# Attention probabilities on their way through DRAM: stores on ScalarE's queue, loads on SyncE's, both in program order

## The chip, the cores and the metric

The kernel runs on one core of a Trainium2 chip. A core has five engines with an instruction stream each: TensorE (PE in the profile, its weight loads as PEld), VectorE (DVE), ScalarE (ACT), GpSimd (POOL) and SyncE (SP). Each stream runs in order. A transfer between memories is an instruction on one of these streams, which only issues it; 16 DMA engines shared by all streams then move the bytes, and the stream goes on. A stream stands still at an instruction whose inputs aren't ready, an issue of a transfer too, and everything behind it on that stream waits as well. The metric is the time of one execution on the device in microseconds, the median of several.

## The reference

Four blocks run after one another: a cross-attention with injected context, a time-mixing layer with a scan, a decoder layer with two attentions, and a non-local block. The change touches the two attentions of the third block, batch 8, sequence 256, width 512, 16 heads of 32:

```python
def attention(q, k, v, mask):
    scores = jnp.einsum('bhqd,bhkd->bhqk', q, k) / jnp.sqrt(jnp.float32(HD))
    scores = scores * mask - 10000.0 * (1.0 - mask)
    probs = jax.nn.softmax(scores, axis=-1)
    return jnp.einsum('bhqk,bhkd->bhqd', probs, v)

ln_out = layernorm(hidden_states, ln1_s, ln1_b)
qkv = ln_out @ w_qkv + b_qkv
q, k, v = jnp.split(qkv, 3, axis=-1)
x = hidden_states + merge_heads(attention(heads(q), heads(k), heads(v), ltor_mask)) @ w_ao + b_ao
ln_out = layernorm(x, ln2_s, ln2_b)
q = ln_out @ w_q + b_q
k, v = jnp.split(encoder_states @ w_kv + b_kv, 2, axis=-1)
x = x + merge_heads(attention(heads(q), heads(k), heads(v), cross_mask)) @ w_co + b_co
```

All of it is computed in float32. The first attention has one mask for all batches, the second a mask and an encoder block per batch.

## The kernel before

**Tiling.** A run i is one batch of one attention: runs 0 to 7 are the first attention (`a_`), runs 8 to 15 the second (`c_`). A run has four iterations, one for each group ct of four heads, so there are 64 iterations; each falls into two halves of two heads. A half is one tile of probabilities, 128 partitions by 4 rows of 256.

**One half** passes through these steps:
- `scores` (L1119, PE): 16 matmuls for the whole iteration, into four PSUM tiles `sp`.
- `masked` (L1131 and L1134, DVE): scale and mask, then add the mask term `mb` and take the row maximum `nmax`; result `pe`.
- `exps` (L1143, ACT): four exponentials with their row sums.
- `divided` (L1151 DVE, L1153 POOL): reciprocals of the sums, then four multiplications on POOL.
- `turn` (L1163 to L1169): DVE transposes `pe` in blocks of 32 by 32 into `dt`; a transfer stores `dt` to a DRAM buffer (L1167, 512 KB of traffic); four transfers load it back from there, with another order of the partitions, into `pt` (L1169, 128 KB each). Each half has a DRAM buffer of its own; `dt` has six buffers, `pt` a tag of its own for each half of an iteration.
- `values` (L1182, PE): 16 matmuls of the iteration with the values `av`. The first four records read the first half's `pt` alone, the other twelve need the second half's as well. ACT moves the result into `cx` (L1186).

**Order.** The main loop (L1278 to L1299) writes, for each step n: the scores of iteration n+1; then for the two halves k of that iteration `masked(k)`, `exps(k)`, `divided(k-1)` and `turn(k-2)`; then other work that has come due; then the values of iteration n-1. The steps of masking, exponentials, division and the transposes are wrapped in `pin`, which is `keep_in_program_order`: among themselves they stay in the order written. A scheduler places everything else among them by its own estimates of times. The stores L1167 and the loads L1169 aren't pinned and are issued from SyncE.

**The other work** of a run, by a table of due times (L1223 to L1234): `at_fetch` loads the run's input `axi` (L1010), `at_norm` and `at_normed` make the LayerNorm (L58 to L61 and L1032 on DVE and ACT, L1034 on POOL, result `axn`), `at_norm_T` transposes it on PE (L83), `at_inputs` loads the second attention's encoder block `enc` (L1019) and mask `mk` (L1021) and computes `mb` from the mask on POOL (L1023), `at_q`, `at_k` and `at_v` are projections on PE (L817, L881) which ACT moves out of PSUM, `at_residual` loads the residual into `hv` or `csx` in turn (L1079) and adds the bias on POOL (L1081, two instructions), `at_out` is the output projection, added on DVE (L1087), and `at_store` stores the run's result (L1093). Weights are loaded at L1628. All these transfers are issued from SyncE. In the attentions the PSUM pool has eight buffers.

Of the kernel before, what the change touches and what calls it, by code (L numbers as in the profile page):

```python
# [621 lines left out]
class Middle:  # L622
# [62 lines left out]
    def plan(self):  # L685
        g, cp, wpool = self.g, self.cp, self.wpool
        nc, I = g.nc, g.I
# [317 lines left out]
        pin = lambda ins: self.tc.keep_in_program_order(ins)  # L1005
# [151 lines left out]
        def turn(i, ct, h2):  # L1157


            pe = t_.pop(("pe", i, ct, h2))  # L1160
            dt = wk.tile([P, 4, S], F32, tag="xn", name="dt", bufs=6)
            pt = t_["pt", i, ct, h2] = wk.tile([P, 4, S], F32, tag=("r", "w4")[h2], name="pt")
            pin(nc.vector.transpose(  # L1163
                dt.rearrange("p c (x q) -> p x c q", q=32), pe.rearrange("p x (k c q) -> p (x k) c q", k=ST, c=4)
            ))
            to = g.dram([4, 32, 4, S], f"pt{i}_{ct}_{h2}")
            nc.sync.dma_start(out=to.rearrange("r k c f -> (r k) c f"), in_=dt)  # L1167
            for c in range(4):
                nc.sync.dma_start(out=pt[32 * c : 32 * c + 32], in_=to[:, :, c].rearrange("r k f -> k r f"))  # L1169

        def values(i, ct):
            pts = [
# [73 lines left out]
        for pre, i, q, kv, o in (("a_", 0, "w_qkv", "w_qkv", "w_ao"), ("c_", B, "w_q", "w_kv", "w_co")):  # L1246
            c = D if q == kv else 0
# [15 lines left out]
        def loop(psums):  # L1263
# [19 lines left out]
            for n in range(-1, len(every)):  # L1283
                if n + 1 < len(every):
                    scores(*every[n + 1])
                for k in (2 * n + 2, 2 * n + 3):
                    if k < len(stream):
                        masked(*stream[k])
                        exps(*stream[k])
                    if 0 < k <= len(stream):  # L1290
                        divided(*stream[k - 1])
                    if 1 < k:
                        turn(*stream[k - 2])
                fill.until(A0 + n + 0.95)
                if n > 0:
                    values(*every[n - 1])
                fill.until(A0 + n + 0.99)
# [458 lines left out]
```

## Time and profile before

| | us |
|---|---|
| median of 3 runs (3466.21 to 3470.12) | 3468.62 |
| the profiled execution | 3462.03 |
| its span | 3460.3 |
| the two attentions, about | 2180 to 2950 |
| PE busy over the span | 3202.3 |
| mean granted clock of PE, share of full speed | 0.964 |

In four stretches of the attentions, busy time of each engine as a share of the stretch, the granted clock and the share of time in which the DMA engines were busy:

| stretch, us | PE | DVE | ACT | POOL | clock | DMA |
|---|---|---|---|---|---|---|
| 2180 to 2380 | 96% | 71% | 62% | 41% | 0.99 | 79% |
| 2380 to 2560 | 90% | 76% | 61% | 41% | 0.95 | 84% |
| 2560 to 2760 | 85% | 72% | 57% | 41% | 0.94 | 78% |
| 2760 to 2960 | 79% | 64% | 50% | 37% | 0.88 | 80% |

A line of waits names the engine that waits, the tile and source line of the waiting instruction, what released it, and then the total in us, the number of waits and the longest. A line of the timeline has the start and the duration in us, the engine, the line, the operation with output and inputs, and the number of instructions run together; SPq is SyncE issuing transfers, whose duration there is that of the issuing and not of the transfer. In brackets stands the idle time before, with what ended it. A line of transfers ends with the size of one and the median time from issue to landing.

### The profile page before, as it was taken

Reading aid. Unit: us, or ns where it says so; the run is one execution under the profiler, and the core shown is the slowest. Engines: PE = TensorE matmul, PEld = TensorE weight load, DVE = VectorE, ACT = ScalarE, POOL = GpSimd, SP = SyncE. Lnnn points to the kernel's source line nnn. Section 1 sums busy time; section 2 is a strip of 40 time slices with the busy share of each in tenths; the row PEclk is TensorE's granted clock in tenths of the full one; section 3 lists DMA queues with packets and bytes.
Section 4 is the critical chain, followed back from the end, with each engine's and each line's share of the span. In section 5 each row is a group of like instructions: output and inputs, shape, how many; then the busy total and the mean of one; then the engine's idle time right before and its main releaser. Section 6 shows DMA issues by size and latency. Waiting matters only on the chain. (4 is left out here: it accounts for less than half of the span.)

```text
span 3460.3 us, 68721 instructions
## 1 busy us (share of the span) xinstructions
PE 3202.3 (93%) x26496; PEld 2286.0 (66%) x26496; DVE 2406.2 (70%) x4175; ACT 1607.7 (46%) x4000; POOL 1663.7 (48%) x1776
## 2 busy tenths in 40 slices
PE   9999999999999998789999997999888887899999
PEld 6677777777777765566566664565555544689996
DVE  5667666666666663888887877667777777677771
ACT  4455555555545564233334333666565554323223
POOL 7533333333323222565566575344343344688872
PEclk9999999999999998899999999999999998899999
DMA  8666665665656533112233332688787778400002
GB/s 276 226 201 194 191 205 181 191 206 187 215 181 194 178 96 129 69 55 98 86 99 103 104 117 76 183 234 241 219 258 225 223 226 243 152 1 1 1 13 85
DMA packets 277365, 533.08 MB, mean 154 GB/s; under 512 B 25056, under 2 KB 153712, under 8 KB 272944
## 3 DMA queue, kind: packets, MB, share of 16 engines
q1 hardware_dynamic: 274144, 523.60, 48.8%
q8 instruction: 211, 3.46, 0.4%
q10 hardware_dynamic: 2224, 3.28, 0.3%
q0 software_dynamic: 672, 1.81, 0.2%
q14 instruction: 114, 0.93, 0.1%
HBM read 411.15 MB, written 117.44 MB: 153 GB/s over the span
## 5 line engine op out<-in xcount | busy, mean ns | idle before, releaser
L391 POOL TENSOR_SCALAR pe<-pe,rinv 128x512 f32<-128x512 f32 x256 | 177.0, 691 | 611.3 <-DVE rinv L390 611.3
L368 DVE TENSOR_REDUCE nmax<-sp 128x2 f32<-128x1024 f32 x256 | 308.9, 1217 | 179.3 <-PE sp L363 179.3
L933 POOL TENSOR_TENSOR rs<-a,r 128x1024 f32<-128x1024 f32 x128 | 303.1, 2383 | 251.9 <-DVE a L928 215.4
L1153 POOL TENSOR_SCALAR pe<-pe,rinv 128x256 f32<-128x256 f32 x512 | 235.1, 478 | 340.2 <-DVE rinv L1151 304.8
L1143 ACT ACTIVATE pe<-pe,nmax 128x256 f32<-128x256 f32 x512 | 255.6, 500 | 224.4 <-DVE nmax L1134 222.3
L377 ACT ACTIVATE pe<-sp,nmax 128x512 f32<-128x512 f32 x512 | 347.0, 683 | 11.2
L403 DVE STREAM_TRANSPOSE pt<-pe 128x1024 f32<-128x1024 f32 x256 | 312.7, 1231 | 24.2 <-POOL pe L391 15.3
L432 PE MATMUL av<-pt,vr 32*64 32x256 f32 x8192 | 262.6, 386 | 39.2 <-issue 31.1
L928 DVE TENSOR_TENSOR_SCAN a<-w,vb 128x1024 f32<-128x1024 f32 x128 | 287.3, 2275 | 4.8
L432 PEld LDWEIGHTS av<-pt,vr 32*64 32x64 f32 x8192 | 211.5, 135 | 102.3 <-issue 61.9
L363 PE MATMUL sp<-k,q 64*64 64x512 f32 x2048 | 267.4, 614 | 5.6 <-ACT pe L377 5.6
L373 ACT ACTIVATE nmax<-nmax 128x2 f32<-128x2 f32 x256 | 51.8, 202 | 402.2 <-DVE nmax L368 401.9
L303 PEld LDWEIGHTS gp<-t,ws 128*128 128x128 f32 x1512 | 185.6, 192 | 30.9 <-issue 13.8
L303 PE MATMUL gp<-t,ws 128*128 128x128 f32 x1512 | 202.9, 278 | 2.2 <-POOL ws L289 1.4
L396 ACT ACTIVATE pe<-pe,rinv 128x512 f32<-128x512 f32 x256 | 182.5, 729 | 40.9 <-DVE rinv L390 40.9
L1182 PE MATMUL cp<-pt,av 128*32 128x256 f32 x1024 | 103.4, 424 | 94.4 <-DMA pt<-pt 83.0
L1163 DVE STREAM_TRANSPOSE dt<-pe 128x1024 f32<-128x1024 f32 x128 | 155.8, 1217 | 14.5 <-POOL pe L1153 14.4
L924 DVE TENSOR_TENSOR vb<-vb,k 128x1020 f32<-128x1020 f32 x128 | 157.2, 1228 | 4.4
L902 PE MATMUL vb<-v,mconstc 32*128 32x255 f32 x1024 | 99.0, 442 | 60.1 <-DVE a L928 60.1
L1435 ACT ACTIVATE h<-h,pvec 128x256 f32<-128x256 f32 x124 | 55.8, 500 | 200.0 <-DVE h L1404 162.7
L1182 PEld LDWEIGHTS cp<-pt,av 128*32 128x32 f32 x1024 | 36.8, 115 | 167.2 <-issue 104.9
L390 DVE RECIPROCAL rinv<-ssum 128x2 f32<-128x2 f32 x256 | 41.1, 160 | 146.7 <-ACT pe L377 146.7
(310 smaller groups left out, 7659.4 us busy)
## 6 DMA issues: line engine op xcount, KB each, us to landing
pt<-dt SPq DMA_DIRECT2D x128, 512.0 KB, 3.3
pt<-pt SPq DMA_DIRECT2D x512, 128.0 KB, 4.4
ws<-sqk SPq DMA_DIRECT2D x110, 512.0 KB, 4.8
wqk<-in_wqk_dram SPq DMA_DIRECT2D x70, 512.0 KB, 5.3
vr<-v SPq DMA_DIRECT2D x128, 256.0 KB, 4.6
ws<-sv SPq DMA_DIRECT2D x56, 512.0 KB, 4.7
wv<-in_wv_dram SPq DMA_DIRECT2D x36, 512.0 KB, 4.8
v<-vT SPq DMA_DIRECT2D x64, 256.0 KB, 2.6
```

Source lines behind the costliest of these rows:

```text
L303: nc.tensor.matmul(out[:, hf * P : (hf + 1) * P], lhsT=w[n](hf, k), rhs=a[n](hf, k), start=k == 0, stop=k == ST - 1,)
L363: nc.tensor.matmul(sp[a * 64 : (a + 1) * 64, h, :], lhsT=qs[b, 2 * un + a][r, ic], rhs=ks[b, 2 * un + a][r, :], start=True, stop=True,)
L368: nc.vector.tensor_reduce(nmax, sp, AX.X, ALU.max, negate=True)
L377: nc.scalar.activation(pe[:, h, :], sp[:, h, :], AF.Exp, bias=nmax[:, h : h + 1], scale=1.0 / DH ** 0.5, accum_out=ssum[:, h : h + 1],)
L391: nc.gpsimd.tensor_scalar(pe[:, 0, :], pe[:, 0, :], rinv[:, 0:1], 1.0, ALU.mult, ALU.mult)
L396: nc.scalar.mul(pe[:, 1, :], pe[:, 1, :], rinv[:, 1:2])
L403: nc.vector.transpose(pts[b, un][:, it], pe)
L432: nc.tensor.matmul(av[r][h * DH : (h + 1) * DH], lhsT=vr[rows_, kb, h * DH : (h + 1) * DH], rhs=pt[rows_, :, h, 32 * kb : 32 * kb + 32], s ...
L928: nc.vector.tensor_tensor_scan(a.rearrange("p n l -> p (n l)"), w4.rearrange("p n l -> p (n l)"), vb[:, 4 * n2 : 4 * n2 + 4, :].rearrange( ...
L933: nc.gpsimd.tensor_tensor(rs, a, rb, ALU.mult)
L1143: pin(nc.scalar.activation(pe[:, r, :], pe[:, r, :], AF.Exp, bias=nmax[:, r : r + 1], scale=-1.0, accum_out=ssum[:, r : r + 1],))
L1153: pin(nc.gpsimd.tensor_scalar(pe[:, r, :], pe[:, r, :], rinv[:, r : r + 1], 1.0, ALU.mult, ALU.mult))
```

## The change

The store of a half goes from SyncE's stream to ScalarE's and is pinned; its four loads stay on SyncE's and are pinned. The pinned instructions of a stream keep the order in which they are written, so on ScalarE the store of half k-2 stands behind the exponentials of half k, and on SyncE the loads of a half stand behind those of the half before. The scheduler lays out the unpinned work of all streams anew around them. Sizes, addresses and the arithmetic are as before.

```diff
             to = g.dram([4, 32, 4, S], f"pt{i}_{ct}_{h2}")
-            nc.sync.dma_start(out=to.rearrange("r k c f -> (r k) c f"), in_=dt)
+            pin(nc.scalar.dma_start(out=to.rearrange("r k c f -> (r k) c f"), in_=dt))
             for c in range(4):
-                nc.sync.dma_start(out=pt[32 * c : 32 * c + 32], in_=to[:, :, c].rearrange("r k f -> k r f"))
+                pin(nc.sync.dma_start(out=pt[32 * c : 32 * c + 32], in_=to[:, :, c].rearrange("r k f -> k r f")))
```

## The prediction

> **What bounds the kernel now.** The change touches one stage, the two attentions, about 2180 to 2950 us of the span. First the page: which engine is full, what the value matmuls (L1182) wait for, and how long the two transfers of the change take.
>
> ```profile
> PE 3202.3 (93%) x26496; PEld 2286.0 (66%) x26496; DVE 2406.2 (70%) x4175; ACT 1607.7 (46%) x4000; POOL 1663.7 (48%) x1776
> ...
> L1182 PE MATMUL cp<-pt,av 128*32 128x256 f32 x1024 | 103.4, 424 | 94.4 <-DMA pt<-pt 83.0
> ...
> pt<-dt SPq DMA_DIRECT2D x128, 512.0 KB, 3.3
> pt<-pt SPq DMA_DIRECT2D x512, 128.0 KB, 4.4
> ```
>
> PE is the bound over the whole, and L1182 is where it waits for the blocks that the change moves: 83.0 us. Next a table of stretches, then the waits of 2180 to 2960 us, then those of SP's own queue.
>
> ```profile
> 2560.00:2760.00 200.00, 170.37 (x966) 102.04 (x967) 143.69 (x426) 114.92 (x358) 81.48 (x155) 0.94 0.78 229
> ```
> ```profile
> POOL pe L1153 <- DVE rinv L1151: 302.2, 94, 9.9
> ACT pe L1143 <- DVE nmax L1134: 205.7, 205, 6.7
> ...
> PE cp L1182 <- DMA pt<-pt: 83.0, 40, 9.6
> ...
> POOL mb L1023 <- DMA mk<-in_mask_b_dram: 37.2, 8, 9.9
> ...
> DVE dt L1163 <- POOL pe L1153: 14.4, 7, 4.1
> ```
> ```profile
> SPq L1167 <- DVE dt L1163: 304.5, 95, 12.0
> SPq L1169 <- DMA pt<-dt: 43.6, 28, 4.2
> ```
>
> In this stretch PE is busy 85%, DVE 72%, ACT 57%, POOL 41% and the transfers 78%: PE bounds it with gaps, and the gaps are a latency chain, transpose, store, four loads, matmul. SP stands 304.5 us at a store whose transpose isn't done; all behind it stands too. The timeline shows an ordinary iteration, then the worst one.
>
> ```profile
> 2711.15 4.38 SPq L1167 DMA_DIRECT2D pt<-dt  x2
> ...
> 2716.11 4.82 SPq L1169 DMA_DIRECT2D pt<-pt  x8
> ...
> 2725.12 1.06 PE L1182 MATMUL cp<-pt,av 128*32 128x256 f32 x12 [0.52 <-DMA pt<-pt]
> ```
> ```profile
> 2572.64 4.45 SPq L1169 DMA_DIRECT2D pt<-pt  x8
> 2577.44 0.40 SPq L1021 DMA_DIRECT2D mk<-in_mask_b_dram  x1
> 2582.13 0.62 POOL L1023 TENSOR_SCALAR mb<-mk 128x512 f32<-128x512 f32 x1 [9.62 <-DMA mk<-in_mask_b_dram]
> 2584.71 1.25 DVE L1163 STREAM_TRANSPOSE dt<-pe 128x1024 f32<-128x1024 f32 x1 [4.12 <-POOL pe L1153]
> 2585.98 6.09 SPq L1167 DMA_DIRECT2D pt<-dt  x2
> 2595.06 3.98 SPq L1169 DMA_DIRECT2D pt<-pt  x8
> 2600.37 1.92 PE L1182 MATMUL cp<-pt,av 128*32 128x256 f32 x12 [8.98 <-DMA pt<-pt]
> ```
>
> Ordinary: both stores, then eight loads; the last twelve value matmuls, which need the second half, wait 0.5 us (0.5 to 1.9 in most iterations). Worst: the mask load stands behind eight loads, POOL waits for it ahead of a division, DVE's transpose is 4.12 us late, and its loads stand behind the next half's store: that store landed at 2590.4, the loads start at 2595.1, 4.7 us later. So the 8.98 us are some 4.3 of POOL's queue and 4.7 of SP's.
>
> **The change, part by part.** The order of instructions of both kernels shows: PE's is the same; 128 stores leave SP for ScalarE, each after the exponentials of the half two ahead; SP keeps loads, half after half; the unpinned work between them falls elsewhere. I number halves from 0; run m holds 8m to 8m+7.
>
> *First half's loads.* They no longer wait for the second store. From the end of a transpose to the last landing, the first half takes 11.9 us (median), the second 10.0, and starts one DVE half (4.05) later, so the second lands 2.2 us after the first and decides. Gain 0; it would show only if the second half came 2.2 us earlier.
>
> *Second half's chain.* Its store now issues while the first half's loads are in flight: 2.6 us in stores alone, 3.0 typical for the second store, 4.3 to 5.4 with loads in flight. That is +1.4; against it its loads have four, not eight, in a row: landing 3.5 to 4.0 for 4.4 to 4.9, so −0.8. Bounds −0.8 to +1.4 per ordinary iteration; I take 0, the ends lying about as near.
>
> *Issue on ScalarE.* 128 issues at 0.34 us are 43.5 us, on an engine 57% busy, which waits 205 times for DVE's nmax; the store waits for a transpose that lies ahead of that nmax on DVE. Behind it queue the evictions of projections (aq, ak, av) and LayerNorm blocks; PE has eight PSUM buffers to run on. Cost 0; without that cover one 0.34 us per iteration, 64 × 0.34 = 22 us.
>
> *The stalls of SP's order* go. In eight runs of the second attention they sit in the period: the first score matmuls of runs 7 to 15 start at 2515.2, 2562.3, 2613.5, 2661.2, 2705.8, 2753.7, 2805.7, 2854.5, 2896.4, so 381.2 us in eight periods, 47.7 each, the cleanest 41.9 (the last), the worst 52.0.
>
> *What the new order adds.* In the second attention SP now issues the residual (hv or csx), enc and mk right after the loads of half 8m+1, and POOL has the two residual adds and mb ahead of the division of half 8m+3, in all eight runs; before, mb alone stood there, in two of them. From the end of transpose 8m+1: store 3.0, pause 0.3, four loads 1.4, so the residual issues at 4.8; it lands 4.9 (csx) to 7.0 (hv) later, mid 10.7; two adds 2.50, mb 0.62, division 1.84, transpose 1.25: 16.9 us (15.9 to 18.0). On schedule two halves are one iteration, 41.9 / 4 = 10.5. The transpose is 6.4 us late (5.4 to 7.5), as the 4.12 above by mb alone, and PE has no slack there. After the 8.98 us stall twelve value matmuls took 1.92 for 1.06 and sixteen scores 2.09 for 1.15; so 0 to 3 more, I take 0.7. Period 41.9 + 6.4 + 0.7 = 49.0, eight are 392.0: **+10.8**. Bounds: 41.9 + 5.4 less 1.9 of ordinary wait is 45.4, −18; 41.9 + 7.5 + 3.0 is 52.4, +38.
>
> *First attention:* the stalls over 2 us at 2445 and 2538 (2.21 + 1.27 + 2.80 + 0.95 = 7.2) are from SP's order in part: **−4.5** (−7.2 to 0). *Tail:* the last half took 15.8 us for a median of 10.0 to 10.4, no PE work follows to hide it: **−3.5** (−5.4 to 0). *Later axn:* three LayerNorms move 4 to 7 halves back on POOL; their scaling 1.51 and the division ahead 1.84 may reach the transposes (L83): 0 to 10, I take 1.5 each, **+4.5**.
>
> Sum: 10.8 − 4.5 − 3.5 + 4.5 = +7.3 on the profiled run's 3462.0 (span 3460.3), 3469.3. The runs' median, 3468.6, is 6.6 above that run; the difference carries: **3476**. Its own range is about 3456 to 3494.
>
> A rule can be set beside the second half's chain. The Trainium skill ("DMA: Bandwidth & Descriptors", section "Issuing engines are not separate DMA queues") says that transfers begun by ScalarE or SyncE run on the same 16 DMA engines and interleave, so that a second issuing engine saves only the issuing time. The rows agree that loads in flight make a store longer (4.3 to 5.4 for 2.6); none here has a store on ScalarE's queue. By the rule alone the change would bring the 0.34 us issues and no more, 0 to −22 us, about 3447 to 3469; it leaves out whose wait stands ahead of whose load, which is what I priced.
>
> **Rivals.** *The waits at L1182 vanish and POOL's new stall does not come* (faster). For: SP is rid of 304.5 us at DVE, so residual and mask may be early. Against: SP now stands at the landing of each store (43.6 us so far, 128 × 3.3 = 422 possible), and the residual stands behind it. If all eight periods became 41.9: 381.2 − 335.2 = 46, with 7.2 and 5.4 it is 58.6: 3410; half of it, 3439.
>
> *Ordinary iterations lengthen* (slower). Place: the second half's store on ScalarE's queue against the first half's loads; price: landing 3.0 to 4.3 or more, of which 0.5 us net in 53 iterations (64 less the 11 with the residual ahead) is +27: 3503. It decides from the point where that half's transpose-to-landing passes 10.0, since PE already waits 0.5 to 1.9 for it. For: transfers already 78% busy here; against: four loads in a row for eight.
>
> *The order does nothing:* excluded, since the two orders differ on SP, ScalarE, POOL and DVE; only the two lines' effect on PE's order is nil.
>
> **How the numbers follow.** Forecast 0.48, vanishing waits 0.24, longer iterations 0.28. A measurement of this kernel tells about 0.2% from no change, 6.9 us. Of the forecast, around +7 with bounds wide on both sides, I put 0.08 faster, 0.18 same, 0.22 slower; vanishing waits all faster but 0.01 the same; the third slower but 0.02 the same: faster 0.31, same 0.21, slower 0.48. The range reaches down to the half-gain (3439, a little under) and up past 3503: 3434 to 3510.
>
> **What would show it.** In the new profile: POOL's wait at L1081 for the residual eight times at 4 to 7 us, DVE's at L1163 for POOL up from 14.4 to some 50; periods of runs 8 to 14 alike near 49; PE's wait for pt still 70 or more but in eight large pieces; the second half's store landing at 4 or more. Wrong if DVE's wait at L1163 stays near 14 (then the first rival), or if the small waits at L1182 grow past 2 us in most iterations (then the second).

## The result, and the profile after

| | before | after |
|---|---|---|
| median, us (20 runs each) | 3462.59 | 3479.41 |
| ratio after to before | | 1.0048, 95% interval 1.0036 to 1.0060 |
| span of the profiled execution | 3460.3 | 3477.4 |

The change makes the kernel 16.8 us slower. The three runs that the prediction stood on had a median of 3468.62; over twenty it is 3462.59, so the forecast of +7.3 is to be held against +16.8.

The starts of the score matmuls and the end of the last value matmul, read from the timeline of both kernels, cut the span into five parts (us). A period here runs from the second iteration of one run to the second iteration of the next: the nine starts that the prediction lists as those of runs 7 to 15 (2515.2 to 2896.4) are the starts of their second iterations.

| part | before | after | difference |
|---|---|---|---|
| up to the first score matmul | 2168.6 | 2172.6 | +4.0 |
| from there to the second iteration of run 7, first attention | 346.5 | 346.4 | −0.1 |
| eight periods, to the second iteration of run 15 | 381.3 | 400.4 | +19.1 |
| from there to the last value matmul | 54.7 | 52.9 | −1.8 |
| the rest | 509.1 | 505.1 | −4.0 |

Cut at the first iterations instead, the eight periods take 381.0 and 398.2 us, so the reading doesn't hang on where they are cut. The first part isn't touched by the change, and it lies between 2165.1 and 2175.4 in the profiles of this study, of kernels with and without it. The periods of the second attention are where the time went. The page of the changed kernel shows the rows that answer to those of before:

```profile
L1163 DVE STREAM_TRANSPOSE dt<-pe 128x1024 f32<-128x1024 f32 x128 | 155.8, 1218 | 72.8 <-POOL pe L1153 72.7
...
L1182 PE MATMUL cp<-pt,av 128*32 128x256 f32 x1024 | 98.3, 428 | 87.2 <-DMA pt<-pt 86.1
...
pt<-dt ACTq DMA_DIRECT2D x128, 512.0 KB, 3.7
pt<-pt SPq DMA_DIRECT2D x512, 128.0 KB, 3.1
```

The loads land in 3.1 us for 4.4, the stores in 3.7 for 3.3; yet PE waits for pt as long as before (86.1 for 83.0), and DVE's transposes wait 72.7 us for POOL where they waited 14.4. The waits of the changed kernel from 2180 to 2975 us, and SP's own, say where that comes from:

```profile
PE cp L1182 <- DMA pt<-pt: 86.1, 29, 7.7
...
DVE dt L1163 <- POOL pe L1153: 72.7, 12, 15.5
...
POOL hv L1081 <- DMA hv<-xa: 38.9, 4, 10.8
...
POOL csx L1081 <- DMA csx<-xa: 30.0, 3, 10.5
```
```profile
SPq L1169 <- DMA pt<-dt: 466.4, 119, 11.5
```

SP no longer stands at a transpose (304.5 us before) but at the landing of each store: 466.4 us, and the residual behind it lands late for POOL. Some lines of the changed kernel's timeline show one such event (start, duration, engine, line, operation; in brackets the wait):

```profile
2635.85 4.06 SPq L1169 DMA_DIRECT2D pt<-pt  x5
...
2639.96 0.43 SPq L1079 DMA_DIRECT2D hv<-xa  x1
...
2640.93 0.51 SPq L1021 DMA_DIRECT2D mk<-in_mask_b_dram  x1
...
2644.29 2.50 POOL L1081 TENSOR_TENSOR hv<-hv,lconstc 128x512 f32<-128x512 f32 x2 [9.28 <-DMA hv<-xa]
...
2648.10 0.62 POOL L1023 TENSOR_SCALAR mb<-mk 128x512 f32<-128x512 f32 x1 [1.31 <-DMA mk<-in_mask_b_dram]
2648.81 3.65 POOL L1153 TENSOR_SCALAR pe<-pe,rinv 128x256 f32<-128x256 f32 x8
...
2650.68 1.25 DVE L1163 STREAM_TRANSPOSE dt<-pe 128x1024 f32<-128x1024 f32 x1 [6.16 <-POOL pe L1153]
...
2662.67 1.92 PE L1182 MATMUL cp<-pt,av 128*32 128x256 f32 x12 [7.73 <-DMA pt<-pt]
```

Read it downwards: residual and mask go out only after the loads of the half before; POOL stands for both, then divides two halves in a row; DVE's transpose is 6.16 us late, and PE's last twelve value matmuls 7.73. Eight such events, one in each of runs 7 to 14, held DVE for 15.49, 6.54, 6.16, 8.63, 4.58, 4.58, 7.42 and 3.60 us, 57.0 together. Two more are alike: one of 6.72 us in the first attention (at 2455, run 5) and one of 7.96 in run 15 (at 2944.75), behind the eight periods, where the residual's adds stand without mb.

The transfers themselves got faster. Medians over the 64 second halves, from the trace's issue and landing times, us:

| step of the second half | before | after |
|---|---|---|
| store, issue to landing | 3.0 | 3.7 |
| landing to first load | 0.34 | 0.06 |
| four loads issued | 1.5 | 1.3 |
| last load issued to last landing | 4.2 | 3.1 |
| end of transpose to last landing | 10.0 | 8.7 |

### The profile page after: what moved, and what is told of

Same layout as the page of the kernel before. It is cut to its first block, busy times and chain, and to the rows that moved or that the text cites. A ratio compares the mean times of both kernels' runs of the same rounds, so it can differ in the third digit from the quotient of the medians.

```text
span 3477.4 us, 68745 instructions
## 1 busy us (share of the span) xinstructions
PE 3209.1 (92%) x26496; PEld 2288.7 (66%) x26496; DVE 2405.0 (69%) x4175; ACT 1607.0 (46%) x4000; POOL 1665.3 (48%) x1776
## 5 line engine op out<-in xcount | busy, mean ns | idle before, releaser
L432 PE MATMUL av<-pt,vr 32*64 32x256 f32 x8192 | 269.0, 394 | 39.7 <-issue 31.0
L373 ACT ACTIVATE nmax<-nmax 128x2 f32<-128x2 f32 x256 | 51.9, 203 | 400.4 <-DVE nmax L368 400.3
L1163 DVE STREAM_TRANSPOSE dt<-pe 128x1024 f32<-128x1024 f32 x128 | 155.8, 1218 | 72.8 <-POOL pe L1153 72.7
L1182 PE MATMUL cp<-pt,av 128*32 128x256 f32 x1024 | 98.3, 428 | 87.2 <-DMA pt<-pt 86.1
L902 PE MATMUL vb<-v,mconstc 32*128 32x255 f32 x1024 | 99.1, 442 | 57.7 <-DVE a L928 57.7
L390 DVE RECIPROCAL rinv<-ssum 128x2 f32<-128x2 f32 x256 | 41.1, 161 | 147.2 <-ACT pe L377 147.2
```

The costliest lines, as they stand in the source:

```text
L432: nc.tensor.matmul(av[r][h * DH : (h + 1) * DH], lhsT=vr[rows_, kb, h * DH : (h + 1) * DH], rhs=pt[rows_, :, h, 32 * kb : 32 * kb + 32], s ...
```

## The experiments

The theory: what costs is that transfers which other work needs stand on SP behind pt loads, which stand at the landing of their stores; the store's move itself shortens the chain. The pins are no part of it: with both pins left out, the instructions of the changed kernel stand in the same order on PE, DVE, POOL and SP, and on ScalarE but for one eviction of cx in the last run, which stands two stores later; with the loads alone pinned, the kernel before has its own order. What reorders the work is the store's engine, through the scheduler. (These are the orders of the programs as built; neither of the two variants was run.) In each experiment PE's order is that of both kernels. A ratio is to the kernel before, with its 95% interval.

**E1 and E2: POOL's other work later.** The adds and mb become steps of their own. E1 has this in the changed kernel, E2 in the one before.

```diff
-            mb = t_["mb", i] = wk.tile([P, ST, S], F32, tag="sq", name="mb")
-            nc.gpsimd.tensor_scalar(mb, mk, 10000.0, -10000.0, ALU.mult, ALU.add)
+        def at_mask(i):
+            mb = t_["mb", i] = wk.tile([P, ST, S], F32, tag="sq", name="mb")
+            nc.gpsimd.tensor_scalar(mb, t_["mk", i], 10000.0, -10000.0, ALU.mult, ALU.add)
...
-            for st in range(ST):
-                nc.gpsimd.tensor_tensor(x[:, st, :], x[:, st, :], g.rv[pre + "bo"], ALU.add)
+        def at_bias(i):
+            for st in range(ST):
+                nc.gpsimd.tensor_tensor(x[:, st, :], x[:, st, :], g.rv[pre + "bo"], ALU.add)
...
-                (-3.1, at_inputs),
+                (-3.1, at_inputs), (-1.4, at_mask),
...
-                (4.1, at_residual),
+                (4.1, at_residual), (5.2, at_bias),
```

> The changed kernel, with the residual's bias adds and the mask term mb put into steps of their own that are due 1.1 and 1.7 iterations after the transfers they need; in the order they now stand one iteration later on POOL, behind the division of half 8m+4 instead of 8m+2. Transfers and queues stay as they are. Theory (POOL stands at transfers that land late, ahead of the division of half 8m+3): DVE's wait at L1163 for POOL falls from 72.7 us to under 20, the eight periods of the second attention from 50.1 to 42 to 44 us, the time to 3415 to 3435, below both kernels. Rival A (the store on ScalarE's queue lengthens ordinary iterations or holds ScalarE up): the time stays at 3470 to 3480. Rival B (the transfers are the limit and only wait elsewhere): DVE's wait falls but PE's wait for pt grows by as much, time 3465 to 3480.

> The kernel before with the same two steps split off. Theory: its POOL waits for mk 37 us and its DVE 14 us at L1163 for POOL; those go, while the waits of SP's order (loads behind the next half's store) stay: 3440 to 3455, so that the change of queue is worth 15 to 30 us once POOL's wait is out of the way in both. Rival A: it is faster than the changed kernel with the split. Rival C (POOL's order alone matters, the queue of the stores nothing): the same time as the changed kernel with the split, within 7 us.

E1: 3453.98 us, ratio 0.9974 (0.9956 to 0.9992). E2: 3444.15, ratio 0.9946 (0.9925 to 0.9968). DVE's wait for POOL at the transposes is gone in E1 (1.9 us in all at L1171, their line there), so POOL's place in the chain was real; but E1 didn't reach 3415 to 3435. E2's time came as expected, though only part of its theory did: POOL's wait for mk fell from 37.2 to 9.1 us, DVE's at the transposes stayed (18.1 for 14.4). E2 is 9.8 us the faster, which is the sign of its rival A (the stores on ScalarE's queue cost of themselves); E5 to E10 bear on that. The waits of E1, from 2180 to 2975 us, show new ones instead:

```profile
POOL axn L1039 <- DVE away L1037: 56.5, 9, 9.2
...
PE cp L1190 <- DMA pt<-pt: 43.5, 23, 4.7
...
PE ln_tp L83 <- POOL axn L1039: 24.4, 22, 3.2
...
DVE hv L1095 <- POOL hv L1089: 19.5, 6, 5.2
DVE csx L1095 <- POOL csx L1089: 17.6, 4, 4.8
...
PE proj L817 <- DMA enc<-in_ctxT_dram: 13.4, 6, 8.4
```

PE's wait for pt is half of what it was (43.5 for 86.1; 71.3 in E2), but now it waits for axn and enc. With mb moved, the scheduler also put the fetch of axi, the input of axn, three halves later on SP. And DVE stands 37.1 us at the output's addition (L1095; none in the changed kernel and in E2) for the bias adds, which now come shortly ahead of it: that part is the place on POOL. So the theory must be wider than POOL's stall at mask and residual; what SP issues late is one candidate, and the adds' new place another.

**E3 and E4: one of the two alone,** in the changed kernel: the upper edit is E3, the lower E4.

```diff
-                (4.1, at_residual),
+                (4.1, at_residual), (5.2, at_bias),
...
-                (-3.1, at_inputs),
+                (-3.1, at_inputs), (-1.4, at_mask),
```

> The changed kernel with the residual's adds alone moved one iteration later; mb stays ahead of the division of half 8m+3. Theory: the mask lands about when the residual does, so the wait stays and only the two adds, 2.50 us, leave the path: eight times 2.5 is 20 us off, 3455 to 3465. If the residual's landing alone were the cause (rival D), it falls as far as with both split, to about 3425.

> The changed kernel with mb alone moved one iteration later; the residual's adds stay ahead of the division of half 8m+3. Theory: 0.62 us off the path per run of the second attention, eight times, 5 us, plus what mb waited beyond the residual (8.1 us in all): 3465 to 3476. If the mask's landing alone were the cause (rival E), it falls to about 3425.

E3: 3479.59 us, ratio 1.0042 (1.0023 to 1.0061). E4: 3481.87, ratio 1.0061 (1.0037 to 1.0084). Both missed. E3 doesn't test what it was to: in the second attention the scheduler put the adds back ahead of the division of half 8m+3, and little but the first attention changed. E4 did move mb; DVE still waits 76.5 us for POOL, since the residual is late and its adds stand in the same place, and axi moved later with mb as in E1 (PE waits 22.5 us at L83). So E4 excludes the mask's landing alone as the cause (rival E); the residual's alone (rival D) is left untested.

**E5 and E6: the other loads on ScalarE.** The edit is shown for the residual; axi, enc and mk have the same. E5 is the changed kernel, E6 the one before.

```diff
-            nc.sync.dma_start(out=x, in_=(g.x2 if pre == "a_" else g.x3)[b])
+            nc.scalar.dma_start(out=x, in_=(g.x2 if pre == "a_" else g.x3)[b])
```

> The changed kernel with the loads of axi, enc, mk and the residual issued from ScalarE too (33 + 8 more issues or so), so that SyncE keeps the pt loads, the results' stores and the weights. PE's order is that of both kernels; POOL now has the residual's adds ahead of the division of half 8m+1 and mb ahead of 8m+7, apart from each other. Theory (SP's standing at the landing of each store makes these loads late, and POOL, then DVE and PE, wait for them): DVE's wait at L1163 for POOL falls from 72.7 us below 30, eight periods of the second attention from 50.1 to 43 to 45.5, time 3420 to 3445. Rival A (ScalarE's queue with the stores costs of itself): it stays above 3455, or above the kernel before with the same edit. Rival B (transfers are the limit): unchanged near 3479.

> The kernel before with the same four loads on ScalarE: stores and pt loads stay on SyncE in the scheduler's order, so the loads of a first half still stand behind the second half's store. Theory: POOL's 37 us for mk go, the second half's chain stays at 10.0 us, against 8.7 in the changed kernel: 3435 to 3455, that is 5 to 25 us above the changed kernel with the same edit. Rival A: it is the faster one of the two, as it was with the split steps.

E5: 3475.22 us, ratio 1.0034 (1.0021 to 1.0048). E6: 3492.24, ratio 1.0087 (1.0071 to 1.0102). The levels missed: ScalarE is a bad place for these loads, in both kernels. But the sign between the two turned, as the theory has it: with these four loads off SP, and mb and axn in the same places on POOL in both kernels, the changed kernel is 17.0 us the faster one. The waits of E5 show what it paid:

```profile
DVE dt L1163 <- POOL pe L1153: 29.1, 14, 3.9
...
ACT ln L88 <- DVE dt L1163: 28.0, 10, 4.3
```

DVE's wait fell as expected (29.1 for 72.7), but ScalarE now stood at stores whose transpose wasn't done, ahead of the evictions of the LayerNorm blocks (ln, 28.0 us; 1.5 in the changed kernel), which PE's projections need. DVE also waits 47.2 us for axi (7.0 in the changed kernel).

**E7 and E8: one queue, strictly in order.** Stores and loads on SyncE, all pinned; E8 with the other loads on ScalarE as well.

```diff
-            pin(nc.scalar.dma_start(out=to.rearrange("r k c f -> (r k) c f"), in_=dt))
+            pin(nc.sync.dma_start(out=to.rearrange("r k c f -> (r k) c f"), in_=dt))
```

> Stores and loads both pinned on SyncE: store, its four loads, next store. The scheduler puts the other transfers between halves differently: axi, mk, enc and the residual in other halves, mb and the adds no longer side by side on POOL. Theory: the second store issues 0.6 us late (3.0 landing, 0.3, 1.4 of issuing against 4.05 of a DVE half), SP stands at landings as in the changed kernel, POOL's stall is spread: 3450 to 3475. Rival A (what costs is ScalarE's queue): clearly faster than the kernel before, below 3445.

> The last one with the loads of axi, enc, mk and the residual on ScalarE. Theory: as the changed kernel with these loads on ScalarE, but the second half's chain is 0.6 us longer, in up to 64 iterations: 0 to 38 us above that, 3430 to 3465. Rival A: below it.

E7: 3566.19 us, ratio 1.0293 (1.0276 to 1.0310). E8: 3562.04, ratio 1.0286 (1.0271 to 1.0302). Both are 100 us slower than the kernel before, far beyond the 0.6 us per iteration expected. The waits of E7, 2180 to 3060 us:

```profile
PE cp L1182 <- DMA pt<-pt: 159.9, 35, 10.7
...
DVE dt L1163 <- POOL pe L1153: 0.7, 2, 0.6
```

POOL holds nobody up here (0.7 us), and still PE waits 159.9 us. The second half's store issues 2.8 us after its transpose (median) and takes 4.6 to land among the first half's loads; its chain is 13.1 us, against 8.7 with the store on ScalarE. This is what the second queue buys: the same order of store and loads without a store behind the loads of the half before. The fixed order on SyncE is also slower than the scheduler's own, where both stores go ahead of the loads (10.0).

**E9 and E10: the transfers due one iteration earlier.** In E9 the residual and the mask leave SP earlier, behind the loads of half 8m-1 instead of 8m+1. The earlier due time of axi only keeps it near its place: it stands behind the loads of half 8m+3, in the changed kernel behind 8m+2. POOL's order in the second attention stays that of the changed kernel. `at_mload` is the mask's load, taken out of `at_inputs`; `at_bias` is that of E1. E10 has the same due times in the kernel before.

```diff
+            e = 0.0 if i < B else 1.0
...
-                (-5.2, at_fetch),
+                (-5.2 - 1 * e, at_fetch),
...
-                (-3.1, at_inputs),
+                (-4.05, at_mload), (-3.1, at_inputs),
...
-                (4.1, at_residual),
+                (3.1, at_residual), (4.1, at_bias),
```

> The changed kernel with three transfers due one iteration earlier: the residual (all runs), the mask and axi (second attention). The adds, mb and axn keep their places: on POOL the order of the second attention is that of the changed kernel, hv or csx and mb ahead of the division of half 8m+3, axn ahead of 8m+7, and PE's order is the same. Only on SyncE the residual and mk now stand behind the loads of half 8m-1 instead of 8m+1 and axi behind 8m+3. Theory (not the place on POOL is the cost, but that SyncE, standing at the stores' landings, issues these transfers too late for it): DVE's wait at L1163 for POOL falls from 72.7 to under 15 us, the eight periods from 50.1 to 43 to 45, the second half's chain stays at 8.7 to 9.5, time 3420 to 3440. Rival F (POOL's work in this place is too long whatever lands when): 3465 to 3480. Rival G (what the second split kernel showed: enc and axn keep PE waiting once POOL is free): 3440 to 3460.

> The kernel before with the same earlier transfers. Theory: POOL's wait for mk goes here too, the second half's chain stays at 10.0 us and the loads of a first half behind the second store: 3435 to 3455, the changed kernel with this edit 5 to 25 us below it. Rival A (the stores on ScalarE's queue cost of themselves): this one is the faster of the two.

E9: 3426.39 us, ratio 0.9892 (0.9873 to 0.9912). E10: 3468.76, ratio 1.0018 (1.0003 to 1.0033). This shows the cause. The adds and mb stand where they cost 57 us of DVE's time in the changed kernel, and only their transfers come earlier; so the place alone isn't the cost (rival F falls), the late issue of residual and mask is. The waits of E9, 2180 to 2960 us, have:

```profile
PE cp L1190 <- DMA pt<-pt: 50.1, 27, 4.5
...
DVE dt L1171 <- POOL pe L1161: 4.5, 3, 3.8
```

SP stands at landings nearly as long as before the edit (399.5 us for 466.4), and DVE hardly waits for what stands behind. The gain lies in the eight periods, 355.8 us for 400.4. They are 57.9, 46.1, 44.1, 39.7, 41.1, 44.5, 40.9 and 41.4: all but the first are below the 49.0 of the same seven in the changed kernel, and four below the best of the kernel before (41.9). E10 missed its range. One event of its timeline shows what the kernel before makes of a small lateness:

```profile
2690.63 0.69 DVE L58 BATCH_NORM_STATS2 ln_stats<-axi 128x6 f32<-128x512 f32 x1 [4.43 <-DMA axi<-xa]
...
2695.20 5.84 SPq L1175 DMA_DIRECT2D pt<-dt  x2
2701.70 5.04 SPq L1177 DMA_DIRECT2D pt<-pt  x8
...
2708.31 1.07 PE L1190 MATMUL cp<-pt,av 128*32 128x256 f32 x4 [4.50 <-DVE rinv L1159]
```

DVE waits 4.43 us for axi ahead of its transposes; the first half's store goes out at 2695.2 and lands 2.7 later, but its loads stand behind the second half's store until 2701.7, 3.8 us after that landing, and PE stands 4.50. Whether all of E10's time comes from such events wasn't taken apart.

**E11: E1 with axi, its statistics and axn one iteration earlier** in the second attention.

```diff
-                (-5.2, at_fetch), (-4.6, at_norm), (-4.1, at_normed),
+                (-5.2 - 1 * e, at_fetch), (-4.6 - 1 * e, at_norm), (-4.1 - 1 * e, at_normed),
```

> The first experiment (adds and mb one iteration later) with axi, its statistics and axn due one iteration earlier in the second attention, so that axn stands ahead of the division of half 8m+7 again instead of 8m+9. Theory: PE's waits at L83 for axn, 24 us there by PE and 36 by its weight loads, mostly go: 10 to 25 us off 3454, 3425 to 3445. If PE's wait for axn hid behind another, the time stays within 7 us of 3454.

3444.95 us, ratio 0.9940 (0.9919 to 0.9962): 9.0 below E1, at the edge of what was expected. PE's wait at L83 fell from 24.4 to 5.7 us, but its wait for pt rose from 43.5 to 60.4, and DVE's at L1095 for the adds stayed (31.2 for 37.1). The time fell by about half of what the wait at L83 lost.

**E12: E9 with the second attention's weights on ScalarE.**

```diff
-            nc.sync.dma_start(out=halves[-1], in_=src[:, i : i + 2, col : col + D])
+            (nc.scalar if name.startswith("c_w") else nc.sync).dma_start(out=halves[-1], in_=...)
```

> The changed kernel with the earlier transfers and with the second attention's weights (c_wq, c_wk, c_wv, c_wo, two transfers of 512 KB each) issued from ScalarE instead of SyncE. It asks what the long period of run 7 is (57.7 us in the changed kernel, where DVE waited 15.49 us, and still 57.9 with the earlier transfers; 40 to 46 in the later periods): six of these transfers fall into it. Theory (SyncE's queue: the weights stand between the mask and the pt loads): the period falls to 46 to 50, the time to 3412 to 3422. Rival B (the bytes: 3 MB more at the 230 GB/s of this stage are 13 us of all DMA engines, whichever queue issues them): the period stays at 54 to 60, the time at 3420 to 3435.

3416.69 us, ratio 0.9874 (0.9857 to 0.9892): the fastest of all, faster than both kernels. The period of run 7 fell from 57.9 to 46.8; the one before it grew from 46.0 to 49.2. Tables of stretches (length, busy us of PE, weight loads, DVE, ACT, POOL; clock, DMA share, GB/s), E9 first and then E12:

```profile
2520.00:2580.00 60.00, 46.99 (x252) 28.64 (x254) 35.20 (x104) 27.91 (x86) 20.28 (x40) 0.83 0.77 238
```
```profile
2520.00:2580.00 60.00, 54.51 (x299) 32.98 (x298) 45.02 (x135) 36.20 (x112) 27.09 (x50) 0.94 0.88 264
```

The DMA engines did more in the same stretch, not less (264 GB/s for 238, a share of 0.88 for 0.77): in E9 they weren't full there, so rival B, the bytes, doesn't explain the long period. But E12 doesn't move the transfers from queue to queue alone: c_wk and c_wv, four of the six, now issue at 2503.7 to 2512.3, ahead of the period (from 2514.1), where in E9 they issue 7.7 to 9.8 us into it. Leaving SyncE's queue and leaving the period aren't told apart.

All pairs with the same edit in both kernels, median us (the scheduler's order of the other work differs within a pair):

| edit | stores on SyncE | on ScalarE | difference |
|---|---|---|---|
| none | 3462.59 | 3479.41 | +16.8 |
| adds and mb later (E2, E1) | 3444.15 | 3453.98 | +9.8 |
| other loads on ScalarE (E6, E5) | 3492.24 | 3475.22 | −17.0 |
| other loads earlier (E10, E9) | 3468.76 | 3426.39 | −42.4 |

## Why the prediction was right, and where not

- **The time.** The forecast was 3476 us and 3479.41 were measured. That these lie 3.4 apart is luck in part: the base of three runs was 6.0 too high, and the change, +7.3 for +16.8, 9.5 too low. The range that the forecast calls its own, 3456 to 3494, isn't worked out; its terms' bounds, added up, give 3438 to 3517.
- **POOL's stall (+10.8): right in mechanism and place.** Counted from the end of transpose 8m+1 as in the sum, in runs 8 to 14 the residual issues after 5.2 to 6.2 us (4.8 was taken, and its three parts give 4.7), lands 4.2 to 5.6 later (4.9 to 7.0), and transpose 8m+3 ends at 16.3 to 18.8 (15.9 to 18.0). DVE's waits there are 3.6 to 8.6, mean 5.9 (a delay of 6.4 was said), and the seven periods are (400.4 − 57.7) / 7 = 49.0, as said. The miss of this term, +19.1 for +10.8, is the first period, 57.7. In run 7 the residual issues after 7.8 us, POOL waits 3.5 more for the mask, and the transpose ends at 23.9: the step "the residual issues at 4.8" left out that the weights stand on SP among these transfers there. DVE's 15.49 us aren't the whole of that period, though: E9, where DVE waits 3.78 there, has 57.9. In E12 11.1 us of it go, with the weights partly moved out of it.
- **The second half's chain (0, bounds −0.8 to +1.4): mis-sized.** It fell by 1.3 us, outside the bounds. The store paid 0.7 where 1.4 was taken, and the loads gained 1.1 in landing, 0.2 in issuing and 0.3 in starting where 0.8 was taken (medians of steps, which don't add up to that of the whole). Part of it belongs to the stalled kernel: with POOL's stalls gone the chain is 9.4 (E1 and E9), against 9.9 to 10.0 with the same edits in the kernel before (E2 and E10), a gain of 0.5, inside the bounds.
- **First half's loads (0): right.** Its chain fell from 11.9 to 9.1 us, but the second half starts 4.05 later and takes 8.7, so it still lands last.
- **Issue on ScalarE (0): right for the change as it is, but not free.** ScalarE's waits for nmax are 204.2 us for 205.7. In four of the eight events an eviction of ak stood 4.7 to 6.6 us, 22.2 together, behind a store whose transpose was late (none before); PE didn't wait for these four. In E5 the evictions of ln stood so, and PE did.
- **First attention (−4.5): wrong,** it was −0.1. The stall at 2445 went, but the residual of run 4 made its own, 6.72 us at DVE at 2455 and 4.61 at PE. **Tail (−3.5):** −1.8, with run 15's 7.96 us at DVE in it. **Later axn (+4.5):** PE waits 7.1 us for axn at L83, none before, at three LayerNorms as said; two of them (4.7 us) lie in the first attention. **Not in the sum:** PE's waits for enc at L817, 9.3 us in four of the eight periods (none before), and the −4.0 after the last value matmul, which the +4.0 ahead of the stage happens to cancel.
- **The signs.** DVE's wait at L1163 rose to 72.7 (some 50 was said) and PE's for pt stayed at 86.1 (70 or more). POOL's waits for the residual were 9.1 to 13.3 us (4 to 7 was said), the second half's store landed in 3.7 (4 or more), and PE's waits for pt of over 3 us came in six of the eight periods, not in all.
- **The rivals.** The vanishing waits came in E9, not here: SP stood at the stores' landings, as was said against them. Longer ordinary iterations fell: the chain got shorter.
- **The rule** (the Trainium skill, "DMA: Bandwidth & Descriptors", section "Issuing engines are not separate DMA queues") holds a second issuing engine to be worth the issuing time alone, by the prediction's estimate 0 to −22 us here. The runs show more than that: a transfer that waits holds those behind it on its engine's stream, 466.4 us of standing on SP in the changed kernel. The same order of stores and loads (E7 and the changed kernel) gives a chain of 13.1 us on one stream and 8.7 on two.

## What to carry to other kernels

In this kernel a transfer that waits for another's landing turns its engine's stream into a standing queue; before it is put there, list everything else that stream issues and when it is needed, and let those go out earlier. The same move was worth +17 us as it stands and −42 with three transfers due earlier in both kernels (−36 against the kernel before as it is). And moving one instruction to another engine lets a scheduler place all the unpinned ones anew: compare the order on every stream, not only at the lines of the diff.

## What the runs showed beyond that

In every profile with the stores on ScalarE the time after the last value matmul is 504.8 to 505.9 us, in every one with them on SyncE 508.7 to 509.5. In the two profiles looked at closely, PE's waits for the weights' sums (ws) at the start of the next stage are 3.6 us (0.7, 0.8 and 2.1) before and 0.6 after; why these sums come earlier wasn't taken apart.
